# The tail of a two-layer image kernel: group-mean operations two strips later, the first turn one strip later, and loads of Fourier modes from the queues of ScalarE and SyncE

## The chip, the cores and the metric

The kernel runs on one core of one Trainium2 chip. The metric is the device time of one execution in microseconds (us); lower is better. The comparison is by the median of several executions.

## The reference

The input x is 4 images of 64 channels of 96 x 96 pixels, float32. Two layers are added to it, each on a group-normalized copy (32 groups, so two channels to a group):

```python
# layer 0: attention with a sigmoid over all 9216 pixels of an image, then a gate for each channel
out = einsum('bcm,bnm->bcn', V, sigmoid(Q^T K)) + v
x = x + out * sigmoid(mlp(mean(out)) + mlp(max(out)))[:, :, None, None]

# layer 1: a layer in Fourier space with 32 x 16 modes
u_hat = rfft2(gn(x))                           # two-dimensional transform of each channel
top = einsum('bchw,cohw->bohw', u_hat[:, :, :16, :16], W_pos)    # complex 64 x 64 mix per mode
bot = einsum('bchw,cohw->bohw', u_hat[:, :, -16:, :16], W_neg)
x = x + irfft2(modes of top and bot, all others zero)
```

## The kernel before, in words

The four images are worked on in two pairs. A pair has 2 x 64 channels, which fill the 128 partitions, and lies in SBUF as one tile of 128 x 9216. Attention over both pairs takes most of the execution: TensorE makes energies (line L572), ScalarE their sigmoids (L593), TensorE the products with the values (L610). The Fourier layer of pair 0 is hidden beside the attention of pair 1 (class `Hidden`). The Fourier layer of pair 1 has nothing to hide beside: it is the **tail**, the code from the pool "tail" on, and takes the last 86 us. The change lies there.

The tail has these stages, in order.

1. **Gate** (L641 to L656), a few small operations, and eight matmul instructions that only keep TensorE busy (`occupy`, L956; there are more such calls later).
2. **Strips.** The pair is cut into 12 strips of 8 image rows (128 x 768). For each strip, VectorE adds layer 0's result to the original x (`combine`, L178), except for the five strips in `ADDED` (4, 5, 6, 8, 10), where ScalarE scales (L975) and a GpSimd DMA accumulates (L976). VectorE then turns the strip (L983, into `xt`, one of four buffers), ScalarE sums its squares (L988), and TensorE makes the transform along the width with six instructions (L995). Strips 0 to 3 share the PSUM tile `pa_0`, 4 to 7 `pa_1`, 8 to 11 `pa_2`; when four are done, `rows_turned(n)` turns the tile on VectorE (L1001, into `a0`, `a1`, `a2`), and `rows(n)` makes the transform along the height (L1007).
3. **Group statistics** (`group_stats`). Means over two channels are made by a matmul with the matrix `pav`. For pair 1, `offset` is that matmul (L146, into the bank `pm`), a copy of its result (L147, into `mr`) and a difference (L148, `d`); `spread_out` (L151) and `third` (L155 to L158, with a power on GpSimd) follow when the variance is there. `spread` (L189 to L203) hands the result to the rows in the order of the modes.
4. **Modes.** VectorE and ScalarE write the modes to the tile `u` (L1042 to L1055). `mix(q, half)`, q from 0 to 7, multiplies four rows of modes by their weights (L225); `evacuate` copies the result from PSUM, in turn by VectorE (L125, half 0) and by ScalarE (L127, half 1). `moved` holds the last copy. For q below 6 the result goes to DRAM by a DMA of SyncE (L243, tensor `vd`) and returns in another layout into the tile `vt` (`back`, L278). The last two q (`NPICK`) never go to DRAM: `pick` moves them by matmuls (L261), and VectorE adds them to `vt` (L266), which needs every load of `vt`.
5. **Inverse transform**: along the height (L1097, `pz`), a turn by VectorE (L1104), along the width (L1114, `py`), the sum with x (L1122) and the stores, in turn from SyncE and ScalarE (L1123).

`back` issues four DMAs for each call, two images by two slots; slot 0 and slot 1 take the queues that it is given in turn. With `queues = (nc.sync, nc.gpsimd)`, the first call (16 rows, 64 KB each) puts all four on GpSimd and the second (8 rows, 32 KB each) two on SyncE and two on GpSimd.

Weights still missing when the tail begins are loaded during the strips: nine of 512 KB by GpSimd into the space of the squares (L1064, each behind the squares of the strips that it overwrites), and eight of 512 KB by SyncE into `a0`, `t0` to `t3`, `a1`, `a2` and `s` (L933, each behind the last matmul that reads its buffer).

The strips, the statistics and the modes stand in `tc.manual_schedule`: each engine takes its instructions in the order written. The mixing loop stands outside of it. `with tc.issue_after(ins)` keeps what is issued inside it on the engine of `ins` behind `ins`; it orders nothing on other engines.

Of the kernel before, what the change touches and what calls it, by code (L numbers as in the profile page):

```python
# [47 lines left out]
KH = 32  # L48
# [35 lines left out]
NPICK = 2  # L84
# [4 lines left out]
def tile_kernel(ctx: ExitStack, tc: tile.TileContext, x, cst, late, spec, out):  # L89
    nc = tc.nc  # L90
# [24 lines left out]
    def named(name, rows=P):  # L115
        return cs[:rows, PLACE[name]]

    pav, nhalf, low_sb, ident = named("pav"), named("nhalf"), named("low"), named("ident")
    turn, moved = [0], [None]

    def evacuate(dst, src):

        turn[0] ^= 1
        if turn[0]:
            moved[0] = nc.vector.tensor_copy(dst, src)  # L125
        else:
            nc.scalar.copy(dst, src)  # L127

    def group_stats(stats, bank, name):


        mv = small.tile([P, 2], F32, tag=f"mv_{name}", name=f"mv_{name}", bufs=1)
        mr = small.tile([P, 2], F32, tag=f"mr_{name}", name=f"mr_{name}")
        t = small.tile([P, 1], F32, tag="t", name=f"t_{name}")
        d = small.tile([P, 1], F32, tag="d", name=f"d_{name}")

        def first():
            nc.vector.bn_aggr(mv, stats.rearrange("p s k -> p (s k)"))

        def second():  # L140
            offset()
            spread_out()

        def offset():
            pm = bank(f"pm_{name}")
            nc.tensor.matmul(pm[:, 0:1], pav, mv[:, 0:1], start=True, stop=True)  # L146
            nc.vector.tensor_copy(mr[:, 0:1], pm[:, 0:1])  # L147
            nc.vector.tensor_tensor(d, mv[:, 0:1], mr[:, 0:1], ALU.subtract)  # L148

        def spread_out():  # L150
            nc.vector.scalar_tensor_tensor(t, d, d, mv[:, 1:2], ALU.mult, ALU.add)  # L151

        def third():
            pv = bank(f"pv_{name}")
            nc.tensor.matmul(pv[:, 0:1], pav, t, start=True, stop=True)  # L155
            ve = small.tile([P, 1], F32, tag="ve", name=f"ve_{name}")
            nc.vector.tensor_scalar(ve, pv[:, 0:1], GN_EPS, None, ALU.add)  # L157
            nc.gpsimd.tensor_tensor(mr[:, 1:2], ve, nhalf, ALU.pow)  # L158

        if stats is None:  # L160
            return mr, [offset, spread_out, third], mv
        return mr, [first, second, third], mv

    def normalize(dst, src, mr):
        nc.vector.tensor_scalar(dst, src, mr[:, 0:1], mr[:, 1:2], ALU.subtract, ALU.mult)

    class Layer1:
# [44 lines left out]
        def mix(self, q, half):  # L212

            pv = self.bank(f"pv_{self.p}_{q}_{half}")  # L220
            for k in range(2):
                kw = half * 2 + k
                for g in range(4):
                    at = ((4 * q + g) * KW + SIDE * kw) * 4
                    self.last = nc.tensor.matmul(  # L225
                        pv[bass.ts(g, 32), :].rearrange("q (n k o) -> q n k o", n=SIDE, o=C)[
                            :, :, k, :],
                        self.ut[:, at:at + 32],
                        self.wts[4 * q + g].rearrange("q (n k o) -> q n k o", n=SIDE, o=C)[
                            :, :, kw, :], start=True, stop=True)  # L230
            vm = self.vms[q].rearrange("q (n m) -> q n m", n=SIDE)
            self.move(vm[:, :, bass.ts(half, 2 * C)], pv.rearrange("q (n m) -> q n m", n=SIDE))
            if half == 0:
                return

            if self.p == 0:
                for g in range(4):
                    self.queues[0].dma_start(
                        self.vd[4 * q + g, :4 * SIDE], self.vms[q][32 * g:32 * g + 4 * SIDE, :])
                if q in (5, 7):  # L240
                    self.back(KH // 2 * (q == 7), KH // 2, self.queues[:1])
            elif q < KH // 4 - NPICK:
                self.queues[0].dma_start(  # L243
                    self.vd[4 * q:4 * q + 4].rearrange("h s m -> (h s) m")[:P - 4 * SIDE],
                    self.vms[q][:P - 4 * SIDE])
                if q == 3:
                    self.vt = self.place_of_vt()
                    nc.gpsimd.memset(self.vt, 0.0)
                    self.back(0, KH // 2, self.queues[1:])
                if q == KH // 4 - NPICK - 1:  # L250
                    self.back(KH // 2, KH // 2 - 4 * NPICK, self.queues)

        def pick(self, picks):

# [167 lines left out]
    with tc.tile_pool(name="work", bufs=1) as work, \  # L422
# [132 lines left out]
        def first_queries():  # L555


            pq = bank_a("pq_first")
            projected[0] = nc.tensor.matmul(pq, named("wq"), xs[0][:, :NB], start=True, stop=True)
            q = qp.tile([P, NB], F32R, tag="q", name="q_first")  # L560

            def splits():
                qu, qh = at[:, 12, :], at[:, 13, :].bitcast(F32R)
                both(qu, qh, pq, named("bq"))
                low_or_high(q, qu, qh, low_sb[:, 0:1])
            return q, splits
# [103 lines left out]
        with tc.manual_schedule(engines=ENGINES):  # L670
# [17 lines left out]
            q, split_queries = first_queries()  # L688
# [108 lines left out]
        while len(done) < len(sizes):  # L797
# [18 lines left out]
            elif total[t] < ALL:  # L816
                steps = together.setdefault(t, [])
# [94 lines left out]
        gate, steps, f = after(1)  # L912
# [7 lines left out]
    with tc.tile_pool(name="tail", bufs=1, reuse_waits="tile") as tail, \  # L920
# [6 lines left out]
        def place_of(tag, name):  # L927

            return tail.tile([P, KW * C], F32, tag=tag, name=name)
# [20 lines left out]
        def occupy(n, behind, pool):  # L950
# [3 lines left out]
            with tc.issue_after(behind.ins):  # L954
                for _ in range(n):
                    nc.tensor.matmul(pd, cs[:, :P], cs[:, :NB], start=True, stop=True)  # L956

        small_bank = psum("ps_m")
        l1 = Layer1(1, gate, lambda name: small_bank.tile([P, NB], F32, tag="m", name=name),
                    evacuate, (nc.sync, nc.gpsimd))  # L960
        l1.wts = wts
        occupy(4, projected[0], small_bank)
        x1 = xs[1]

        mr, steps, mv = group_stats(None, l1.bank, "l1_1")
# [32 lines left out]
        def rows_turned(n):  # L998

            a = place_of(f"a{n}", f"a_{n}")  # L1000
            nc.vector.transpose(a, along_w[n].rearrange("q (h c) -> q c h", c=SQ))  # L1001
            along_h[n] = a.rearrange("q (c s k) -> q s c k", s=2, k=KW)

        def rows(n):
            for part in range(2):
                for b in range(2):
                    nc.tensor.matmul(pu[b], fh[bass.ts(b, C), part, bass.ts(n, P)],  # L1007
                                     along_h[n][bass.ts(b, C), part],
                                     start=(n == 0 and part == 0),
                                     stop=(n == NSQ - 1 and part == 1))  # L1010
# [9 lines left out]
        with tc.manual_schedule(engines=ENGINES):  # L1020
            for s in range(NSTRIP):
                if s not in ADDED:
                    l1.combine(s, again[:, bass.ts(s, STRIP)])
                strip(s)
                if s == 1:
                    steps[0]()
                if s == 4:
                    rows_turned(0)
                    rows(0)
                if s == 9:  # L1030
                    rows_turned(1)
            var = small.tile([P, 1], F32, tag="var", name="var")
            nc.vector.tensor_reduce(var, squares, AX.X, ALU.add)
            nc.vector.tensor_scalar(mv[:, 1:2], var, 1.0 / N, None, ALU.mult)
            steps[1]()
            steps[2]()
            rows_turned(2)
            rows(1)
            rows(2)
            l1.spread(mr)  # L1040
            for b in range(2):
                nc.vector.transpose(t[:, bass.ts(b, NB)],  # L1042
                                    pu[b].rearrange("q (c k) -> q k c", k=KW))
            for half in range(2):
                h = bass.ts(half, KH // 2)
                for b in range(2):
                    nc.scalar.activation(u[:, :, :, h, 0, b], tb[b][:, :, :, h], AF.Copy,
                                         scale=l1.rs[:, 0, b:b + 1])
                    nc.vector.tensor_scalar(u[lo, :, :, h, 1, b], tb[b][hi, :, :, h],
                                            l1.rs[hi, 1, b:b + 1], None, ALU.mult)  # L1050
                    if b == 0:
                        nc.vector.tensor_scalar(u[hi, :, :, h, 1, b], tb[b][lo, :, :, h],
                                                l1.rs[lo, 0, b:b + 1], None, ALU.mult)
                    else:
                        nc.scalar.activation(u[hi, :, :, h, 1, b], tb[b][lo, :, :, h], AF.Copy,  # L1055
                                             scale=l1.rs[lo, 0, b:b + 1])
                if half == 0:
                    l1.constant_mode()
# [164 lines left out]
```

## Time and profile before

| what | us |
|---|---|
| median of 3 runs (lowest, highest) | 3034.89 (3033.67, 3035.25) |
| the profiled execution's own time | 3035.74 |
| its span in the profile | 3033.9 |
| start of the tail: attention's last matmul ends | 2948.19 |
| first combine, strip 0 (L178) | 2951.38 |
| last matmul of strip 11 ends (L995) | 2978.08 |
| mixing, first to last matmul of L225 | 2985.06 to 2999.08 |
| addition into `vt` starts (L266) | 3006.25 |
| inverse transform along the height starts (L1097) | 3007.77 |
| inverse transform along the width starts (L1114) | 3016.67 |

Times are microseconds from the start of the span. The profiled execution took 1.84 us more than its span, and 0.85 us more than the median. In a line of the trace's timeline the columns are the start, the duration, the engine, the line, the operation, output and input with their shapes, and how often; in brackets stands how long the engine was idle before, and what released it. POOL is GpSimd, DVE is VectorE, ACT is ScalarE, SP is SyncE, PE is TensorE and PEld its weight load. "SPq" or "POOL" with DMA_DIRECT2D is the issue of a DMA, not its transfer. PEclk is the TensorE clock that was granted, as a share of full speed.

### The profile page before, as it was taken

Reading aid. Unit: us, or ns where it says so; the run is one execution under the profiler, and the core shown is the slowest. Engines: PE = TensorE matmul, PEld = TensorE weight load, DVE = VectorE, ACT = ScalarE, POOL = GpSimd, SP = SyncE. Lnnn points to the kernel's source line nnn. Section 1 sums busy time; section 2 is a strip of 40 time slices with the busy share of each in tenths; the row PEclk is TensorE's granted clock in tenths of the full one; section 3 lists DMA queues with packets and bytes.
Section 4 is the critical chain, followed back from the end, with each engine's and each line's share of the span. In section 5 each row is a group of like instructions: output and inputs, shape, how many; then the busy total and the mean of one; then the engine's idle time right before and its main releaser. Section 6 shows DMA issues by size and latency. Waiting matters only on the chain.

```text
span 3033.9 us, 44107 instructions
## 1 busy us (share of the span) xinstructions
PE 3011.3 (99%) x19364; PEld 1114.1 (37%) x19364; DVE 308.4 (10%) x706; ACT 2416.9 (80%) x1555; POOL 73.1 (2%) x144
## 2 busy tenths in 40 slices
PE   9999999999999999999999999999999999999998
PEld 4333333333333333333433333333333333333336
DVE  6300000000000000002411101000000000000006
ACT  4788888888888888887788887778778888888872
POOL 0100000000000000001200000000001000000001
PEclk9999999999999999999999999999999999999999
DMA  4100000000000000001423222421113000000027
GB/s 160 31 4 4 4 4 4 4 4 4 4 1 4 4 4 4 4 4 37 108 53 78 76 79 88 132 39 39 56 41 125 4 4 4 4 4 4 6 68 238
DMA packets 114401, 117.09 MB, mean 39 GB/s; under 512 B 77520, under 2 KB 84496, under 8 KB 114112
## 3 DMA queue, kind: packets, MB, share of 16 engines
q1 hardware_dynamic: 105536, 92.82, 11.1%
q0 software_dynamic: 7664, 18.89, 2.0%
q8 instruction: 152, 2.49, 0.3%
q10 hardware_dynamic: 1008, 2.56, 0.2%
q14 instruction: 41, 0.34, 0.0%
HBM read 79.94 MB, written 32.31 MB: 37 GB/s over the span
## 4 chain that ended last, share of the span: by engine, by line
PE 97%; DVE 1%; DMA 1%; issue 0%; ACT 0%; SPq 0%; POOL 0%; DVEq 0%; POOLq 0%; ACTq 0%
PE banks L610 77%; PE banks L572 17%; PE banks L491 1%; PE banks L225 1%; DVE x L1122 0%; PE banks L413 0%; PE pa L995 0%; DMA x<-in_x_dram 0%; ACT at L593 0%; PE pv L225 0%; PE pz L1097 0%; PE banks L336 0%; PE pu L1007 0%; PE banks L456 0%; DVE xt L983 0%
## 5 line engine op out<-in xcount | busy, mean ns | idle before, releaser
L593 ACT ACTIVATE at<-banks 128x2048 f32<-128x2048 f32 (+1 forms) x1501 | 2388.3, 1642 | 532.0 <-PE banks L572 520.3
L610 PE MATMUL banks<-at,vT 128*64 128x512 f32 (+1 forms) x11824 | 2400.6, 546 | 0.0
L610 PEld LDWEIGHTS banks<-at,vT 128*64 128x64 f32 x11824 | 777.8, 136 | 1361.8 <-issue 1306.8
L572 PE MATMUL banks<-q,kT 32*128 32x512 f32 x5040 | 542.6, 452 | 0.8 <-ACT at L593 0.7
L572 PEld LDWEIGHTS banks<-q,kT 32*128 32x128 f32 x5040 | 223.7, 182 | 447.5 <-issue 337.4
L616 DVE SCALAR_TENSOR_TENSOR x<-banks,x 128x512 f32<-128x512 f32 x36 | 24.9, 691 | 2023.3 <-PE banks L610 1945.4
L542 POOL DMA_DIRECT2D stage<-qk x96 | 47.7, 504 | 930.6 <-DMA qk<-turned 928.8
L417 DVE TENSOR_TENSOR x<-banks,x 128x768 f32<-128x768 f32 x12 | 11.5, 958 | 168.5 <-PE banks L413 168.5
L491 PEld LDWEIGHTS banks<-cs,x 64*64 64x64 f32 x1152 | 21.8, 135 | 16.6 <-ACT at L593 11.5
L498 DVE TENSOR_TENSOR vT<-banks,cs 128x256 f32<-128x256 f32 x72 | 26.8, 413 | 0.0
L491 PE MATMUL banks<-cs,x 64*64 64x80 f32 (+1 forms) x1152 | 25.9, 234 | 0.0
L618 DVE TENSOR_REDUCE maxs<-x 128x1 f32<-128x512 f32 x36 | 24.7, 686 | 1.3
L624 DVE BATCH_NORM_STATS2 stats<-x 128x6 f32<-128x512 f32 x36 | 22.6, 681 | 3.7 <-DMA x<-in_x_dram 3.7
L728 DVE COPY ws<-banks 128x512 f32<-128x512 f32 x16 | 11.1, 692 | 115.3 <-PE banks L225 115.3
L158 POOL TENSOR_TENSOR mr_l<-ve_l,cs 128x1 f32<-128x1 f32 x4 | 2.2, 562 | 840.2 <-DVE ve_l L157 840.2
L995 PE MATMUL pa<-xt,lc 128*128 128x256 f32 x72 | 18.3, 410 | 3.0 <-DVE xt L983 3.0
L976 POOL DMA_DIRECT2D x<-vT x5 | 4.4, 1001 | 659.3 <-ACT x L975 659.3
L728 DVE COPY ae<-banks 128x512 f32<-128x512 f32 x6 | 4.2, 692 | 157.3 <-issue 114.9
L663 PE MATMUL banks<-x 128*128 128x256 f32 (+1 forms) x48 | 14.2, 451 | 4.9 <-DMA x<-in_x_dram 4.7
L572 PE MATMUL banks<-q_first,kT 32*128 32x512 f32 x144 | 17.1, 459 | 1.7 <-ACT at L593 1.1
L988 ACT ACTIVATE vT<-x,less 128x768 f32<-128x768 f32 x12 | 11.1, 926 | 9.4 <-DVE x L178 7.3
L529 DVE STREAM_TRANSPOSE turned<-t 128x384 f32<-128x384 f32 (+1 forms) x35 | 17.8, 510 | 1.2
(146 smaller groups left out, 440.7 us busy)
## 6 DMA issues: line engine op xcount, KB each, us to landing
ws<-in_spec_dram SPq DMA_DIRECT2D x20, 512.0 KB
q<-qk SPq DMA_DIRECT2D x280, 32.0 KB
x<-in_x_dram SPq DMA_DIRECT2D x17, 512.0 KB
out_dram<-x SPq DMA_DIRECT2D x17, 384.0 KB
room<-in_spec_dram SPq DMA_DIRECT2D x12, 512.0 KB
old<-in_x_dram SPq DMA_DIRECT2D x12, 384.0 KB
qk<-turned SPq DMA_DIRECT2D x96, 48.0 KB
x1d<-x SPq DMA_DIRECT2D x12, 384.0 KB
```

Of the source, the lines that this page charges most:

```text
L225: self.last = nc.tensor.matmul(pv[bass.ts(g, 32), :].rearrange("q (n k o) -> q n k o", n=SIDE, o=C)[:, :, k, :], self.ut[:, at:at + 32], s ...
L491: projected[0] = nc.tensor.matmul(pp[bass.ts(e, P // 2), b, 2 * a + h, :width], src[rows, a, h, bass.ts(e, P // 2)], named("wv")[rows, :wi ...
L498: nc.vector.tensor_tensor(vT[:, 4 * s:4 * s + 4, bass.ts(b, C)].rearrange("p (h a) m -> p a h m", h=2), pp[:, b, :, :C].rearrange("p (a h) ...
L529: nc.vector.transpose(turned[:, k:].rearrange("p k a (m h) -> p (k a) h m", h=2), t[:, k:].rearrange("p k a h m -> p (k a) h m").bitcast(F32))
L542: nc.gpsimd.dma_start(come[bass.ts(r, QK), :], split[p][s][:, r % 2, bass.ts(r // 2, NB // 2)])
L572: nc.tensor.matmul(banks[:, bank_of(i), :], kT[r:r + 32, i % TILES // 8, i // 4 % 2, :], ask[i // TILES][r:r + 32, :], start=True, stop=True)
L593: nc.scalar.activation(at[:, of:of + n, :], banks[:, bank:bank + n, :], AF.Sigmoid)
L610: attended[0] = nc.tensor.matmul(acc[half, cols], vT[:, j, half], at[:, place(2 * pair + b), cols], start=(j == 0), stop=(j == NCH - 1 and ...
L616: nc.vector.scalar_tensor_tensor(blk, acc, 1.0, blk, ALU.mult, ALU.add, accum_out=sums[p][:, m:m + 1])
L618: mark[0] = nc.vector.tensor_reduce(maxs[p][:, m:m + 1], blk, AX.X, ALU.max)
L624: each = [lambda s=s: nc.vector.bn_stats(stats[:, s, :], xs[p][:, bass.ts(s, NB)]) for s in range(NBLK)]
L995: nc.tensor.matmul(along_w[n][:, bass.ts(i, STRIP // NSQ)], fw[:, bass.ts(k, P)], v[:, k], start=(k == 0), stop=(k == NSQ - 1))
```

## The change

The matmul of `offset` becomes a step of its own, `shared`, which stays behind strip 1; the copy and the difference that remain in `offset` move behind strip 3. `rows_turned(0)` and `rows(0)` move from behind strip 4 to behind strip 5. In pair 1, the first call of `back` moves from behind `mix(3, 1)` to behind `mix(6, 1)` and the second from behind `mix(5, 1)` to behind `mix(7, 1)`; the queues become SyncE and ScalarE. So the first call's four DMAs are ScalarE's, behind ScalarE's copy for q = 6, and the second's are two of SyncE and two of ScalarE, the latter behind ScalarE's copy for q = 7. The clearing of `vt` (L248) stays where it is. The diff:

```diff
-    turn, moved = [0], [None]
+    turn, moved = [0], [None, None]
...
         if turn[0]:
             moved[0] = nc.vector.tensor_copy(dst, src)
         else:
-            nc.scalar.copy(dst, src)
+            moved[1] = nc.scalar.copy(dst, src)
...
         def second():
+            shared()
             offset()
             spread_out()
 
+        pm = []
+
+        def shared():
+            pm.append(bank(f"pm_{name}"))
+            nc.tensor.matmul(pm[0][:, 0:1], pav, mv[:, 0:1], start=True, stop=True)
+
         def offset():
-            pm = bank(f"pm_{name}")
-            nc.tensor.matmul(pm[:, 0:1], pav, mv[:, 0:1], start=True, stop=True)
-            nc.vector.tensor_copy(mr[:, 0:1], pm[:, 0:1])
+            nc.vector.tensor_copy(mr[:, 0:1], pm[0][:, 0:1])
             nc.vector.tensor_tensor(d, mv[:, 0:1], mr[:, 0:1], ALU.subtract)
...
         if stats is None:
-            return mr, [offset, spread_out, third], mv
+            return mr, [shared, offset, spread_out, third], mv
...
                 if q == 3:
                     self.vt = self.place_of_vt()
                     nc.gpsimd.memset(self.vt, 0.0)
-                    self.back(0, KH // 2, self.queues[1:])
-                if q == KH // 4 - NPICK - 1:
-                    self.back(KH // 2, KH // 2 - 4 * NPICK, self.queues)
+            if self.p == 1 and q >= KH // 4 - NPICK:
+                with tc.issue_after(moved[1].ins):
+                    if q == KH // 4 - NPICK:
+                        self.back(0, KH // 2, self.queues[1:])
+                    else:
+                        self.back(KH // 2, KH // 2 - 4 * NPICK, self.queues)
...
-                    evacuate, (nc.sync, nc.gpsimd))
+                    evacuate, (nc.sync, nc.scalar))
...
                 strip(s)
-                if s == 1:
-                    steps[0]()
-                if s == 4:
+                if s in (1, 3):
+                    steps[s // 2]()
+                if s == 5:
                     rows_turned(0)
                     rows(0)
...
-            steps[1]()
             steps[2]()
+            steps[3]()
             rows_turned(2)
```

## The prediction

> **What bounds the kernel now.** I began with the page's busy shares: TensorE has 99% of the span, but nearly all of that is attention, which the diff leaves alone. So I went to the chain that ended last, from 2948 us on, to see what carries the tail:
>
> ```profile
> 2954.86 2.59 PE pa L995 x12
> 2957.45 0.13 PE pm_l L146 x2
> ...
> 2957.61 0.17 DVE mr_l L147
> ...
> 2961.87 4.23 PE pa L995 x12
> 2966.10 0.04 issue
> 2966.14 1.99 PE pu L1007 x8
> ...
> 2981.83 0.33 PE pr L189 x8
> ```
>
> The columns are start, duration and what. The chain goes back and forth between TensorE and VectorE: neither is the bound of the strips, each waits for the other. The timeline names the waits:
>
> ```profile
> 2957.61 0.16 DVE L147 COPY mr_l<-pm_l 128x1 f32<-128x1 f32 x1 [1.97 <-PE pm_l L146]
> 2959.95 1.67 PE L995 MATMUL pa<-xt,lc 128*128 128x256 f32 x6 [2.38 <-DVE xt L983]
> 2961.87 4.23 PE L995 MATMUL pa<-xt,lc 128*128 128x256 f32 x12 [0.24 <-DVE xt L983]
> 2964.83 1.25 DVE L1001 STREAM_TRANSPOSE a<-pa 128x1024 f32<-128x1024 f32 x1 [2.16 <-PE pa L995]
> ```
>
> VectorE idles 1.97 us at the copy of `pm`, whose matmul stands behind the twelve of strips 0 and 1; TensorE then has no strip for 2.38 us; and VectorE idles 2.16 us for `pa_0`. The third line shows a cost that no wait shows: twelve instructions take 4.23 us here, against 2.59 above. The windows of 1 us (length; busy time of PE, PEld, DVE, ACT, POOL; then PEclk, DMA share, GB/s) say why:
>
> ```profile
> 2958.00:2959.00 1.00, 0.00 (x0) 0.00 (x0) 0.96 (x2) 0.08 (x1) 0.32 (x1) 1.00 1.10 194
> 2963.00:2964.00 1.00, 1.00 (x4) 0.82 (x3) 0.00 (x0) 1.00 (x3) 0.01 (x1) 0.50 1.16 151
> 2965.00:2966.00 1.00, 1.00 (x6) 0.62 (x4) 1.00 (x1) 0.00 (x0) 0.45 (x1) 1.00 0.91 314
> 3005.00:3006.00 1.00, 0.00 (x0) 0.00 (x0) 0.00 (x0) 0.00 (x0) 0.00 (x0) 0.83 0.03 8
> 3008.00:3009.00 1.00, 1.00 (x6) 1.00 (x8) 0.00 (x0) 0.00 (x0) 0.00 (x0) 0.50 0.00 0
> ```
>
> The idle TensorE lost half its clock from 2961.3 to 2964.7, and again from 3005.7 to 3012.4. The second loss follows the loads of `vt`:
>
> ```profile
> 2998.00 0.56 POOL L278 DMA_DIRECT2D vt<-vd  x1 [10.04 <-DMA vd<-vm]
> 3000.33 1.30 SPq L278 DMA_DIRECT2D vt<-vd  x2
> 3001.42 2.65 POOL L278 DMA_DIRECT2D vt<-vd  x5 [2.86 <-issue]
> 3006.25 1.42 DVE L266 TENSOR_TENSOR vt<-picked,vt 128x256 f32<-128x256 f32 x4 [7.28 <-DMA vt<-vd]
> ```
>
> GpSimd issues one load at 2998.00, stands 2.86 us with nothing shown as the cause, and issues the other five until 3004.07. The last, issued at 3003.51, lands 2.33 us later; only then does VectorE add. The picks were done at 3002.7, so this stage waits for GpSimd's queue alone.
>
> [...] the four switches (2961.34, 2964.69, 3005.67, 3012.45) lie 3.35, 40.98 and 6.78 us apart, multiples of 3.4. In both windows ahead of a drop TensorE was idle some 2.05 us. [...] the trace's SyncE loads moved their bytes by 3002.9, though no landing is shown for them. [...]
>
> **Part 1: `offset` behind strip 3, the first turn behind strip 5.** No operation is added or removed. I ran both queues forward with steps from this trace: combine to turn 1.01 us, turn to next 0.90, `rows_turned` 1.18, copy and difference 0.27 together; on TensorE 1.37 per strip at full clock (the first twelve instructions took 2.75 in the timeline) and 1.83 for `rows(0)` (half of the 3.63 to 3.70 of sixteen).
> VectorE: turn of strip 1 at 2954.66, combine 2 at 2955.56, turns of 2 and 3 at 2956.57 and 2958.48, copy at 2959.36 (its matmul was done at 2957.57: no wait), turns of 4 and 5 at 2959.63 and 2960.50, `rows_turned(0)` at 2961.37.
> TensorE: strip 2 from 2957.60, strip 3 from 2959.46 to 2960.83, which is before VectorE wants `pa_0`. TensorE's gap is 0.49 us in place of 2.38, so I expect no loss of clock. From there it is the bound: 9 strips at 1.37 and `rows(0)`, 14.16 us, from 2959.46 to 2973.62, against 2977.9 before. The matmul of the variance (L155) follows at once: **4.28 us earlier**. The accumulated strips don't stop this: issued from 2952.61 on, they land after 4.0 to 10.2 us, strip 4 by 2956.6, strip 6 by 2961.1, strip 10 by 2966.1, each ahead of its turn (2959.63, 2962.6, 2969.3). Moved past: ScalarE's squares and GpSimd's loads follow the strips and come earlier too. If that cover failed (an accumulation later), the cost would be its lateness, at most the 4.28.
>
> The loads of weights cannot come earlier in bulk: the DMA share is about 1 from 2965 to 2986. The only slack is 2973 to 2976, some 1.1 us at 410 GB/s. So they drain near 2985.4 (2986.5 less 1.1) and the last one, for `s`, near 2986.7. `mix` would then start at 2980.8 and want its last rows at 2992.8: covered by 6 us. But the writes to `vd`, 6 x 459 KB, would begin behind the drain and move some 0.32 MB per us (windows 2990 to 2993): 8.6 us, to 2995.3, and 0.9 to land. Unhindered, the last would land at 3000.30 - 4.28 = 2996.0. I take 0.5 us for this crowding, 0 to 2 as its bounds.
>
> **Part 2: the loads of `vt`.** Times here are before the shift of 4.28. ScalarE's copy for q = 6 ends at 2997.99, and the first four rows of `vd` landed at 2997.36, so its four issues start at once. No row shows ScalarE issuing small loads of 1 KB runs. Its stores (L1123) take 0.34 us each, SyncE's two loads of this kind 0.28 and 0.97, SyncE's 280 loads L550 0.30 to 2.00 with a median of 0.42. I take the median: 4 x 0.42 = 1.7 us, bounds 1.2 and 8.0. Queued behind them is ScalarE's copy for q = 7, for which `pick` waits: it moves from 2999.14 to 2999.7 and ends at 3000.3. TensorE is with the picks of q = 6 until 3000.87, so nobody waits. The second call's loads may go when the last `vd` row has landed (3000.30): SyncE's as before, ScalarE's at 3000.4 and 3000.8. SyncE's later one, issued at 3000.66, moved its bytes by 3002.9; with four at once I put the last landing at 3003.4. So L266 starts at 3003.45 instead of 3006.25: **2.8 us earlier**, 2.3 after the crowding. GpSimd loses six DMAs and nothing waits for it any more; late next is a tie of the loads and of the picks (3002.7).
>
> **Part 3: the clock.** TensorE would be idle from 3003.6 to 3004.9, 1.3 us and not 4.2, less than the 2.05 us that cost the clock. At full speed `pz` takes half its 6.13 us. VectorE's first turn then starts 1.05 us after TensorE instead of 2.07, and its eight turns run without their 0.39 us gap. Before `py` stand six busy-keeping instructions of 2.84 us that wait for about the fifth turn: 1.05 + 5 x 0.67 + 0.1 + 2.84 = 7.35 against 8.90 before. **1.5 us**, from 0 (clock lost again) to 2.5 (that wait is not binding). The last stage is VectorE's 13 sums and is unchanged.
>
> **Sum.** 4.28 + 2.3 + 1.5 = 8.1 us off the profiled execution: span 3025.8, time 3035.74 - 8.1 = 3027.6. That execution stood 0.85 above the median, so from 3034.89 I get 3026.8.
>
> **Rivals.**
> - *Part 1 alone holds.* ScalarE's issues take 0.97 each: its copy ends at 3002.5, the picks at 3004.4, the second call's loads land near 3005.2; 0.9 us minus crowding is gained and the clock falls again. 3034.89 - 4.3 - 0.4 = 3030.2. For it: SyncE's 0.97 on this very kind of load. Against it: stores at 0.34. Likewise 3030.6 if nothing but the strips moves.
> - *The transfers give the 4.28 back.* If the drain of weights, not TensorE, sets when `vd` lands, 3000.30 stays and only parts 2 and 3 count: 3034.89 - 2.8 - 1.5 = 3030.6. For it: the share of 1 to 2986. Against it: `mix` never waits for a weight, and the last write is bound by its own issue.
> - *Slower: ScalarE's queue becomes the bound.* With d for an issue, L266 starts at 2997.99 + 6d + 0.58 (the copy) + 1.7 (landing). It breaks even with 3006.25 at d = 1.0, and with the strips' 4.28 at d = 1.71. At the longest SyncE issue seen, 2.00, it starts at 3012.3, 6.0 later than before: 3034.89 - 4.28 + 6.0 = 3036.6. For it: nothing shows this queue in such use. Against it: a mean at the worst of 280.
> - *It doesn't do what it says:* the mixing loop is outside the written order, so the planner may put ScalarE's copy for q = 7 ahead of the first loads. Then all six follow 2999.72, the last landing is near 3004.3 and 1 us of the gain is lost: 3027.8.
>
> **How the numbers follow.** The full case with the planner's variant 0.61 (3024.8 to 3028.8), the two rivals near 3030.5 together 0.30, one in six of that at 3028.8 or less when a part of the clock is kept, ScalarE's queue 0.09. About 0.2%, 6.07 us, is what a measurement can tell from no change; the border is 3028.8. Faster: 0.61 + 0.05 = 0.66. Slower by over 0.2% (3041.0) needs d above 2.7: 0.04 of the 0.09. Within: 0.30. The range reaches from the full case's low end (strips 4.4, loads 3.3, clock 2.4) to 3031.2, beyond the rivals near 3030.5.
>
> **What would show it.** Right: no idle of VectorE at L147 and L1001, PEclk 1.00 from 2957 to 2966; L155 near 2973.6; L225 starting near 2980.8; eight `vt` issues on ACTq and SPq, four behind the copy for q = 6; L266 near 2999.7, L1097 near 3001.1 with PEclk 1.00, L1114 near 3008.5. Wrong: ACT copies of L127 late by over 1.2 us with the picks waiting for them, weights awaited by L225, or `vd` landing as late as 3000.

## The result, and the profile after

The median of 18 runs fell from 3035.06 to 3028.64 us; the ratio is 0.998, with a 95% interval from 0.9973 to 0.9988. That is 6.4 us or 0.21%, inside the range that was forecast and 1.8 us slower than the forecast number. By the interval the gain is 3.6 to 8.2 us: that the kernel became faster is clear of noise, that it did so by more than 0.2% is not. The profiled execution has a span of 3027.4 us and took 3029.19, so it stands 0.55 above the median. The changed kernel's runs lie from 3027.40 to 3031.39 in two groups, nine up to 3028.09 and nine from 3029.19 on. The median falls into the gap between them, where no run stands; one run more in either group would move it by 0.55 us.

The same chain of waits as before, from the strips on (start, duration, what; line numbers are those of the changed kernel, up to eight higher):

```profile
2961.12 0.05 DVE mr_l L152
2961.17 0.00 issue
2961.17 4.15 PE pa L1003 x18
2965.32 1.92 PE pu L1015 x8
2967.24 2.80 PE pa L1003 x12
...
2982.69 14.02 PE pv L230 x256
2996.71 3.65 PE picked L269 x16
3000.36 0.87 PE idle_I-15684_15689 L964 x2
```

Where 12 instructions of L1003's counterpart took 4.23 us, 18 now take 4.15. The timeline shows the two waits gone and the loads on their new queues:

```profile
2961.04 0.12 DVE L152 COPY mr_l<-pm_l 128x1 f32<-128x1 f32 x1
2963.03 1.21 DVE L1009 STREAM_TRANSPOSE a<-pa 128x1024 f32<-128x1024 f32 x1
2975.55 0.28 PE L160 MATMUL pv_l<-t_l,cs 128*128 128x1 f32 x2
2995.33 1.99 ACTq L286 DMA_DIRECT2D vt<-vd  x4
2997.36 0.58 ACT L127 COPY w_early<-pv 128x512 f32<-128x512 f32 x1 [1.74 <-PE picked L269]
2997.67 0.81 ACTq L286 DMA_DIRECT2D vt<-vd  x2
2997.77 0.63 SPq L286 DMA_DIRECT2D vt<-vd  x2
3001.34 1.42 DVE L274 TENSOR_TENSOR vt<-picked,vt 128x256 f32<-128x256 f32 x4 [4.75 <-PE idle_I-15684_15689 L964]
3002.86 3.92 PE L1105 MATMUL pz<-vt,gh_in_fours 64*128 64x256 f32 x32 [1.64 <-DVE vt L274]
3003.99 4.90 DVE L1112 STREAM_TRANSPOSE z<-pz 128x512 f32<-128x512 f32 x8 [1.24 <-PE pz L1105]
3006.71 2.84 PE L964 MATMUL idle_I-15718_15732<-cs 128*128 128x512 f32 x6
```

No bracket stands behind the copy and the turn: VectorE no longer waits there. ScalarE's four issues take 1.99 us and end at 2997.32; its copy for q = 7 follows at 2997.36 (its bracket names the picks, but it stands behind these issues in ScalarE's queue), and the two SyncE issues go when the last row of `vd` has landed. The windows (the third column from the right is the granted clock) hold the surprise:

```profile
28.00:29.00 1.00, 1.00 (x6) 0.27 (x4) 0.00 (x0) 1.00 (x1) 0.00 (x0) 0.50 0.24 59
2963.00:2964.00 1.00, 1.00 (x6) 0.89 (x5) 1.00 (x2) 0.92 (x3) 0.54 (x1) 1.00 1.05 187
3004.00:3005.00 1.00, 1.00 (x12) 0.94 (x11) 1.00 (x2) 0.00 (x0) 0.00 (x0) 1.00 0.00 0
```

In the tail the clock is full as long as TensorE works, as forecast (1.00 in every window of 1 us from 2950 to 3020). But it was halved at 28 us, where the first profile of before had 1.00, and all that follows came late: attention's last matmul ended at 2949.81 instead of 2948.16. From there to the end of the span the tail took 85.74 us before and 77.59 after, 8.15 less, almost the 8.1 of the sum. The medians differ by 6.4. The experiments ask where the difference comes from.

### The profile page after: what moved, and what is told of

The parts are those of the page before. It is cut to its first block, busy times and chain, and to the rows that moved or that the text cites. A ratio compares the mean times of both kernels' runs of the same rounds, so it can differ in the third digit from the quotient of the medians.

```text
span 3027.4 us, 44108 instructions
## 1 busy us (share of the span) xinstructions
PE 3009.2 (99%) x19364; PEld 1111.5 (37%) x19364; DVE 308.1 (10%) x706; ACT 2416.8 (80%) x1555; POOL 69.8 (2%) x138
## 3 DMA queue, kind: packets, MB, share of 16 engines
q0 software_dynamic: 7472, 18.56, 2.0%
q10 hardware_dynamic: 1408, 2.88, 0.3%
## 4 chain that ended last, share of the span: by engine, by line
PE 98%; DVE 1%; DMA 0%; ACT 0%; issue 0%; SPq 0%; POOL 0%; DVEq 0%; ACTq 0%
PE banks L618 77%; PE banks L580 17%; PE banks L499 1%; PE banks L230 1%; PE pv L230 0%; DVE x L1130 0%; PE banks L421 0%; DMA x<-in_x_dram 0%; PE pa L1003 0%; ACT at L601 0%; PE banks L344 0%; PE pu L1015 0%; PE banks L464 0%; DVE xt L991 0%; DVE x L183 0%
## 5 line engine op out<-in xcount | busy, mean ns | idle before, releaser
L170 DVE TENSOR_SCALAR x<-x,mr_l 128x512 f32<-128x512 f32 x36 | 17.6, 530 | 0.7 <-POOL mr_l L163 0.7
L1003 PE MATMUL pa<-xt,lc 128*128 128x256 f32 x72 | 16.8, 385 | 0.6 <-DVE mr_l L152 0.4
```

## The experiments

Stages are measured in each profile: *strips* from the first combine to the variance's matmul, *loads* from the start of mixing to the addition into `vt`, *pz* from the first matmul of the transform along the height to that along the width, *stores* from the last sum to the end of the span. *Attention* is the end of its last matmul, and *tail* is the time from there to the end of the span. Every line is one execution. Each text set apart below is what was expected of an experiment: a theory, and its rivals.

| profile | attention | tail | strips | loads | pz | stores |
|---|---|---|---|---|---|---|
| before | 2948.16 | 85.74 | 26.53 | 21.19 | 8.83 | 5.44 |
| after | 2949.81 | 77.59 | 22.52 | 18.65 | 6.62 | 6.05 |
| before again | 2949.89 | 84.61 | 26.24 | 20.75 | 8.31 | 5.56 |
| after again | 2949.90 | 77.90 | 22.52 | 18.89 | 6.62 | 6.13 |
| strips' part alone | 2948.17 | 81.93 | 22.51 | 20.99 | 9.12 | 5.55 |
| loads' part alone | 2948.25 | 81.75 | 26.24 | 19.12 | 6.71 | 5.93 |
| before, busy behind the picks | 2948.17 | 84.23 | 26.07 | 20.77 | 6.43 | 5.88 |
| before, pair near 25 us | 2948.15 | 83.75 | 25.17 | 20.58 | 8.31 | 5.93 |
| after, pair near 25 us | 2948.47 | 77.63 | 22.51 | 18.70 | 6.62 | 6.04 |
| the same, trimmed | 2948.65 | 78.25 | 22.51 | 18.91 | 6.93 | 6.15 |
| after, early places | 2949.90 | 81.50 | 22.52 | 22.97 | 6.62 | 5.64 |
| after, SyncE alone | 2949.72 | 82.18 | 22.52 | 20.37 | 9.36 | 6.18 |
| after, first turn at strip 4 | 2948.52 | 78.08 | 22.83 | 18.61 | 6.62 | 6.27 |
| after, pair near 25, two behind the picks | 2948.36 | 77.64 | 22.52 | 19.07 | 6.62 | 5.68 |

**Both kernels once more**, unchanged.

> The kernel before, unchanged, for a second profile. In its first profile the tail took 85.7 us from the last attention matmul to the end; in the changed kernel's profile 77.6, so 8.2 us less, though the medians of all runs differ by 6.4. Theory A (chance of the clock): [...] the same kernel loses it in other places in another execution; this tail then differs from 85.7 by over 0.5 us, and a stage with a clock of 0.50 has moved, gone or been added. Theory B (fixed): the tail is again 85.7 within 0.3 us and the difference to the medians comes only from the 1.5 us lost near 27 us in the changed kernel's profile.

> The changed kernel, unchanged, for a second profile. In its first one TensorE ran at half clock from 26.8 to 31 us, which the kernel before did not in its own, and everything from there to the tail came 1.65 us later. Theory A: the loss at 27 us is chance, and this profile need not have it; the attention then ends near 2948.2 as before. Theory B: it belongs to the changed program, and attention ends again near 2949.8. Both expect a tail of 77.6 us within 0.5[...].

The kernel before again, windows:

```profile
28.00:29.00 1.00, 1.00 (x4) 0.24 (x2) 0.00 (x0) 1.00 (x1) 0.00 (x0) 0.50 0.24 59
2963.00:2964.00 1.00, 1.00 (x4) 0.81 (x3) 1.00 (x2) 1.00 (x3) 0.12 (x1) 0.50 1.07 200
3008.00:3009.00 1.00, 0.24 (x2) 0.27 (x3) 0.66 (x2) 0.00 (x0) 0.00 (x0) 1.00 0.02 8
3010.00:3011.00 1.00, 1.00 (x6) 0.84 (x6) 1.00 (x2) 0.00 (x0) 0.00 (x0) 0.50 0.00 0
```

Now the kernel before has the early half clock too, ends attention at 2949.89, and has a tail 1.1 us shorter than in its first profile. Its second loss begins between 3009 and 3010, behind the start of the transform along the height at 3008.76 and not 2.1 us ahead of it. Theory A holds for the tail of before. What repeats is the length of the losses: 3.35 and 6.78 us in the first profile of before, 3.42 near 28 us in that of the changed kernel (worked out from the clock of its windows at 26 and 30 us, 0.84 and 0.95), and, worked out in the same way, 3.40 to 3.42 or 6.82 in the five experiments below whose windows show both ends. So each loss is as long as one or two steps of about 3.4 us, while its place in the work differs between the executions. The changed kernel's second profile has the early loss again (attention ends at 2949.90, which is what its Theory B said); since the kernel before now has it too, it does not belong to the changed program alone. Its tail, 77.90, is what both theories expected.

**Each part alone.** The strips' part alone keeps the old loads; the loads' part alone keeps the old strips:

```diff
 # strips' part alone, against the changed kernel: the two calls of back as in the kernel before, and
-                    evacuate, (nc.sync, nc.scalar))
+                    evacuate, (nc.sync, nc.gpsimd))
 # loads' part alone, against the kernel before: back behind mix(6, 1) and mix(7, 1), and
-                    evacuate, (nc.sync, nc.gpsimd))
+                    evacuate, (nc.sync, nc.scalar))
```

> Only the part in the strips: offset behind strip 3, first turn behind strip 5; loads of vt as before, from GpSimd and SyncE. The prediction's sum gives it 4.3 us (4.0 in the changed kernel's profile, from first combine to the variance's matmul), so a ratio near 0.9986 and a median near 3030.8. Rival (clock is part of the price): of the 4.3 us some 1.5 is the half clock from 2961 to 2965 in the one profile of before, and executions without it gain only 2.5 to 3, a ratio near 0.9991.

> Only the part in the loads: back behind mix 6 and 7, from ScalarE and SyncE; strips as before. The prediction's sum gives it 2.3 us for the loads and 1.5 for the clock in the transform along the height, 3.8 in all, a ratio near 0.9987. Rival (clock by chance): executions of before that keep the clock there gain 2.5 only, a ratio near 0.9992. If the two parts are independent, the gains of this kernel and of the strips alone add up to that of both, about 6 to 6.4 us.

Medians of 13 runs: 3032.64 and 3033.09, against 3035.11; both ratios are 0.9993, with intervals from 0.9985 to 1.0001 and to 1.0002. So 2.5 and 2.0 us, near the rivals and below the sum's 4.3 and 3.8; but the intervals reach from no gain to one of 4.6 us, so they don't exclude the sum's values either. The two gains add up to 4.5 us, not to the 6 to 6.4 that were expected of independent parts; intervals this wide leave open whether the parts need each other. By stages they are independent: each brings its own stage about to the length that it has in the changed kernel (22.51, and 19.12 where the profiles with both parts have 18.6 to 19.1) and leaves the other as before. What they do not fix is the clock: the strips' part alone had its pz at 9.12, the longest but one, with a clock of 0.50 from 3003 to 3008, and the loads' part alone still lost the clock in the strips, where 13 instructions took 4.20 us (12 take 2.86 at full clock, as a profile below shows).

**The clock by itself**: the kernel before with TensorE kept busy behind the picks.

```diff
-        occupy(1, l1.last, mix_bank)
+        occupy(7, l1.last, mix_bank)
```

> The kernel before, with seven pairs of busy-keeping matmuls behind the picks instead of one, so that TensorE is not idle while VectorE waits for the loads; nothing else. Theory (the clock is a part of the gain by itself): PEclk stays 1.00 through the transform along the height, from its first matmul to that along the width 6.6 us instead of 8.3 to 9.1, the addition still starts with the loads, and the median falls by about 2 us, to 3033. Rival (the addition waits for the busy-keeping matmuls too, as the changed kernel's profile says of its one pair): it starts a little later than the loads, and the gain shrinks to 1.5 or less. Rival (the clock isn't the cause of the 2.2 us): the stage keeps its 8.3 to 9.1.

The median was 3035.46, ratio 0.9999 (0.9991 to 1.0008): no gain that can be told, where 2 us were expected. The timeline of this kernel says why:

```profile
3002.12 6.17 PE L956 MATMUL idle_I-15684_15689<-cs 128*128 128x512 f32 x14
3005.38 1.42 DVE L266 TENSOR_TENSOR vt<-picked,vt 128x256 f32<-128x256 f32 x4 [6.86 <-DMA vt<-vd]
3008.22 3.72 PE L1097 MATMUL pz<-vt,gh_in_fours 64*128 64x256 f32 x32
```

The theory's mechanism is there: at full clock (1.00 in every window from 3000 to 3020) the 32 instructions take 3.72 us instead of 6.13, and pz 6.43. But my fourteen instructions ran 6.17 us, beyond the addition, and the transform waited 1.3 us behind them. I had taken too many; so this run prices the clock at 1.9 to 2.4 us in pz, of which 0.6 to 1.1 would be left behind that wait, too little for the medians to show. The addition starts while they run: it doesn't wait for them.

**The early loss.** One pair of matmuls into a bank that the next energies overwrite, at a time when TensorE waits for the first sigmoids (1.06 us in the first profile of before), in the kernel before and in the changed one:

```diff
             values_of(0, 1)()
+            warm(0, NB)
```

> The kernel before, with one pair of busy-keeping matmuls near 25 us, where TensorE idles for the first sigmoids. Theory (the early half clock is chance, worth 1.65 us where it strikes): PEclk is 1.00 from 22 to 40 us, attention ends at 2948.2, and the runs lie closer together than the 3032.5 to 3037.6 of before; the median falls by 0.3 to 1 us. Rival: the spread has another cause and stays.

> The changed kernel with the same pair near 25 us. Theory: attention ends at 2948.2, the two groups of run times (3027.4 to 3028.1, and 3029.2 to 3031.4) become one near 3027.5, and against the kernel before with the same pair it is faster by the 7.4 us that four profiles give for the tail (85.7 and 84.6 before, 77.6 and 77.9 after). Rival (the tail's gain is really about 6): the difference of the two is 6 us or less.

The clock is 1.00 at 28 us in both, and attention ends at 2948.15 and 2948.47. All four profiles with the pair end it by 2948.65; of the ten without it five end it at 2949.72 or later. Medians: 3034.49 and 3028.11, so 6.4 us between the two, and the tails of 83.75 and 77.63 differ by 6.1: nearer to the rival's 6 than to the theory's 7.4. The changed kernel's 9 runs lie from 3027.71 to 3029.99, not in one group yet: two stand near 3029.9. The kernel before went from 3035.22 to 3034.49, not clear of noise (ratio 0.9997, 0.9989 to 1.0005), and its 13 runs still spread over 4.1 us against 5.2 of 33 runs without the pair, so most of its spread has another cause, as the rival said. Here the tail of the kernel before was the shortest of the three seen, and this is what it looks like:

```profile
2957.60 0.16 DVE L147 COPY mr_l<-pm_l 128x1 f32<-128x1 f32 x1 [1.97 <-PE pm_l L146]
2959.94 1.56 PE L996 MATMUL pa<-xt,lc 128*128 128x256 f32 x6 [2.38 <-DVE xt L984]
2961.86 2.86 PE L996 MATMUL pa<-xt,lc 128*128 128x256 f32 x12 [0.35 <-DVE xt L984]
2963.45 1.25 DVE L1002 STREAM_TRANSPOSE a<-pa 128x1024 f32<-128x1024 f32 x1 [0.79 <-PE pa L996]
```

TensorE was idle for the same 2.38 us as in the kernel before, yet the clock stayed full (1.00 at 2961 and at 2963), and the twelve instructions took 2.86 us, not 4.23. VectorE's second wait shrank from 2.16 to 0.79. So of the 4.0 us that the strips' part takes from the first profile, 1.36 go with the clock and 2.66 (25.17 less 22.51) are there without it.

**Fewer busy-keeping matmuls ahead of the last transform**, on top of the pair near 25 us:

```diff
-        occupy(3, last, py_bank)
+        occupy(1, last, py_bank)
```

> The same as the changed kernel with the pair near 25 us, and one pair of busy-keeping matmuls instead of three ahead of the transform along the width. In the changed kernel's profile these six instructions end at 3009.5, 0.6 us after VectorE's last turn at 3008.9. Theory: that transform starts right behind the last turn, 0.5 us sooner, and the median is 0.5 us under that of the kernel with three. Rival: TensorE's idle time there costs the clock, the sums of the last stage come later, and it is slower by 1 us or more.

The median was 3028.02, ratio to the kernel before 0.9974 (0.9965 to 0.9984), against 3028.11 and 0.9977: no difference that can be told. The profile can't be compared by its length, since this execution lost the clock at about 3003.1, ahead of the edit, early in a transform along the height before which TensorE had been idle for 1.9 us:

```profile
3004.00:3005.00 1.00, 1.00 (x8) 1.00 (x7) 0.80 (x2) 0.00 (x0) 0.00 (x0) 0.50 0.00 0
```

The theory's first half is there: the transform along the width starts at 3008.88, 0.06 us behind VectorE's last turn, and so pz is 6.93 in spite of the lost clock.

**The old places with the new queue**: in the changed kernel, `back` again behind `mix(3, 1)` and `mix(5, 1)`, without `issue_after`.

```diff
-            if self.p == 1 and q >= KH // 4 - NPICK:
-                with tc.issue_after(moved[1].ins):
...
+                    self.back(0, KH // 2, self.queues[1:])
+                if q == KH // 4 - NPICK - 1:
+                    self.back(KH // 2, KH // 2 - 4 * NPICK, self.queues)
```

> The changed kernel with ScalarE and SyncE as queues, but back at its old places (behind mix 3 and mix 5) and without the order behind ScalarE's copies. The planner then puts the first call's four loads behind ScalarE's copy for q = 4, ahead of that for q = 5. Theory (the places matter because ScalarE's waiting issue holds its copies): the loads wait for the fourth row of vd, which lands 12.3 us after mixing starts; four issues of 0.5 follow; the copies for q = 5, 6 and 7 come 3.5 us late, with them the last write to vd, and L274's counterpart starts 21 to 22 us after the start of mixing, not 18.7 to 18.9. Rival (the queue alone makes the gain): 18.7 to 19.2 here too.

ScalarE's rows:

```profile
2991.67 0.58 ACT L127 COPY w_early<-pv 128x512 f32<-128x512 f32 x1 [1.12 <-PE pv L230]
2995.76 2.67 ACTq L283 DMA_DIRECT2D vt<-vd  x4
2998.47 1.56 ACT L127 COPY w_early<-pv 128x512 f32<-128x512 f32 x3 [6.21 <-DMA vt<-vd]
3002.16 0.81 ACTq L283 DMA_DIRECT2D vt<-vd  x2
```

ScalarE stands 6.2 us between its copies, three of them come at once, the last write to `vd` goes 16.31 us after the start of mixing instead of 11.23, and the addition starts 22.97 us after it. The theory's direction and its mechanism hold; its 21 to 22 was too low, because the wait ended at 13.0, not 12.3, and an issue took 0.67. TensorE waited 2.80 us for those copies, and its clock was halved during the picks (0.50 from 3001 to 3003), which took 5.41 us instead of 3.72; but the addition starts 3.6 us after the second call's first issue, as in the changed kernel (3.7), so it is the loads that set it. In this stage the queue alone costs 2 us against before (22.97 against 21.19); with the new places it gains 2 (18.65 to 18.89).

**The new places with SyncE alone**:

```diff
-                    evacuate, (nc.sync, nc.scalar))
+                    evacuate, (nc.sync, nc.sync))
```

> The changed kernel with all eight loads of vt on SyncE. The planner puts one load of the first call between the writes to vd for q = 4 and q = 5. Theory (it waits for the fourth row's landing, 12.3 us after mixing starts, and holds the last write by 1.2 us): that lands near 16.4, four more issues of 0.4 to 0.6 follow, and the addition starts 20 to 21 us after the start of mixing. Rival (any hardware queue does it): 18.7 to 19.2, as with ScalarE.

SyncE's rows:

```profile
2992.11 0.30 SPq L248 DMA_DIRECT2D vd<-w_early  x1
2995.67 0.32 SPq L286 DMA_DIRECT2D vt<-vd  x1
2996.10 0.36 SPq L248 DMA_DIRECT2D vd<-w_early  x1
2996.51 4.16 SPq L286 DMA_DIRECT2D vt<-vd  x7
```

The first load sits waiting between the two last writes, holds the second until 13.51 us after the start of mixing (11.23 in the changed kernel), and the addition starts at 20.37, inside the theory's 20 to 21. What the rival calls a hardware queue stands in the list of queues of the two first profiles: from before to after, q0, named software_dynamic, falls from 18.89 to 18.56 MB and q10, named hardware_dynamic, rises from 2.56 to 2.88 MB, by about the 0.33 MB of the six loads that went from GpSimd to ScalarE; SyncE's transfers are in q1, hardware_dynamic too. So it is not enough to take any hardware queue. `issue_after` orders nothing on SyncE, since it names ScalarE's copy; whether SyncE would do with its loads kept behind the last write was not tried.

**The first turn back behind strip 4**, the rest as changed:

```diff
-                if s == 5:
+                if s == 4:
```

> The changed kernel with the first turn back behind strip 4: of the strips' part only the offset moves. From the first combine to the variance's matmul the kernel before took 26.2 to 26.5 us with half clock near 2961 and 25.2 without it, the changed one 22.5. Theory (the two edits take away one wait each): the offset gives back its 2.0 us wait and the clock, the turn still waits for TensorE, and the stage takes 22.9 to 23.5. Rival (the turn's wait came from the late strips 2 and 3, so it is gone with the offset's): 22.5 to 22.7, the second edit is worth nothing.

```profile
2961.49 1.25 DVE L1009 STREAM_TRANSPOSE a<-pa 128x1024 f32<-128x1024 f32 x1 [0.53 <-PE pa L1003]
```

The strips took 22.83 us, 0.31 more than with the turn behind strip 5, between the rival's 22.5 to 22.7 and the theory's 22.9 to 23.5. VectorE's wait for `pa_0` is still there, 0.53 us of the 2.16. So in this one profile the offset's move does nearly all of it, and most of the turn's wait came from the late strips 2 and 3, as the rival said, but not the whole.

**A version that keeps the clock**: the pair near 25 us and one more pair behind the picks.

```diff
-        occupy(1, l1.last, mix_bank)
+        occupy(2, l1.last, mix_bank)
```

> The changed kernel with the pair of busy-keeping matmuls near 25 us and a second pair behind the picks, so that TensorE's idle time ahead of the transform along the height is 0.7 us instead of 1.6. Theory (an idle time of 1.6 us loses the clock in some executions, as the trimmed kernel's profile shows, and the addition doesn't wait for these matmuls): the runs near 3030 are gone, the median is 3027.5 to 3028, and the stage from that transform to the next is 6.6. Rival (the addition waits for them): it starts 0.9 us later, and the median is 3028.5 or more.

```profile
2998.74 1.88 PE L965 MATMUL idle_I-15685_15690<-cs 128*128 128x512 f32 x4
3000.30 1.42 DVE L274 TENSOR_TENSOR vt<-picked,vt 128x256 f32<-128x256 f32 x4 [5.17 <-DMA vt<-vd]
```

The median of 9 runs was 3027.77, ratio 0.9974 (0.9964 to 0.9984), and they lie from 3027.40 to 3028.27, as the theory said. The addition began at 3000.30 while the second pair ran until 3000.62, so it doesn't wait for it. TensorE was idle for 1.21 us ahead of the transform, not 0.7, and pz is 6.62. The idle time that lost the clock in the trimmed kernel's profile was 1.90 us; that 1.6 does it too was my estimate and is not shown. The median is 0.9 below that of the changed kernel, and its slowest run is faster than half of the changed kernel's; but the two were measured at different times, and the intervals of their ratios overlap. That it is the second pair that takes the runs near 3030 away is not shown: without it, with the pair near 25 us, they were two of nine, and in the trimmed kernel, also without it, none of nine.

## Why the prediction was right, and where its size was off

- **The strips.** Right in every step: the turn of strip 3 was forecast at 2958.48, 7.10 us after the start of the first combine (2951.38), and measured at 2960.14, 7.11 after 2953.03; TensorE back to back from there; no wait at the copy. Measured 4.01 and 3.72 us in the first two pairs of profiles, against 4.28; the forecast counted the clock lost there as a part of the gain, and against the profile that kept it the part is worth 2.66. The missing 0.3 of the first pair is for the most part the last strip, for which TensorE waits after all (0.23 us): VectorE and TensorE end nearly together.
- **Crowding of the DMA engines.** The first pair shows none: SyncE's wait for the last row of `vd` ends 15.08 us after the start of mixing, against 15.27 before. But over all profiles with the copies on time it ends after 14.6 to 15.3 with the loads at their old places (five profiles, mean 14.89) and after 15.1 to 15.6 with them at the new ones (seven, mean 15.35). So some 0.5 us is lost after all, and not for the reason given: the strips' part alone has 14.70, the loads' part alone 15.63. It goes with the loads' new places, not with the weights that were moved; how is not shown.
- **The loads.** 2.8 forecast ahead of that crowding and 2.3 with it, 2.54 measured in the first pair and 2.1 as a mean of three profiles of each kernel, with and without the pair near 25 us (20.8 before, 18.7 after). ScalarE's issue, the unknown, was 0.50 us against the 0.42 chosen from SyncE's loads, far below the 1.71 at which the slower rival would have broken even; its copy for q = 7 started 14.67 us after mixing, forecast 14.64. The planner kept the order.
- **The clock.** 1.5 forecast; 2.21 and 1.69 measured. The sum let the six busy-keeping instructions ahead of `py` wait for about the fifth turn, 4.50 us after the start of `pz`. They do not wait for it: they start at 3006.71, 3.85 us after that start and right behind the last `pz` matmul (3006.78), and pz is 6.62 and not 7.35. Nor do the 32 `pz` instructions take half of 6.13 us: 3.72 to 4.01 in the profiles with full clock there. The other step, that idle time below 2.05 us (TensorE's in the 3.4 us ahead of each of the first profile's two drops) keeps the clock, is refuted as a bound. It held in the changed kernel's own tails (1.64 and 1.88 us idle; forecast 1.3), but 1.90 us lost the clock in the trimmed kernel and 2.10 kept it with the loads' part alone, and near 25 us an idle time of 1.07 us was followed by half clock. So what kept the clock in these tails is not shown.
- **The stores** were put down as unchanged, with VectorE's 13 sums as the last stage. The sums are unchanged (10.62 and 10.63 us); the time behind the last one is 5.4 to 6.3 us in the profiles, 6.1 in the mean of the changed kernel's first two against 5.5. What decides that is open.
- **What was off is the sum's base.** It took one profile's losses of the clock for a fixed price, and took 8.1 us from the median as if every execution paid it. The tail of before was 85.74, then 84.61, then 83.75 in the version with the pair near 25 us, and the forecast was made from the dearest of the three. The changed kernel's three are 77.59, 77.90 and 77.63. So the three pairs differ by 8.15, 6.71 and 6.12 us, 7.0 in the mean. That the first came so near to 8.1 is in part luck: 4.01, 2.54 and 2.21, less 0.61 for the stores, stand where the sum had 4.28, 2.3, 1.5 and nothing. Whether the early loss of 1.65 us makes up the rest of the distance to 6.4 is not shown. It struck one of four profiles made from the kernel before without the pair and four of six made from the changed kernel, too few to tell; and with the pair in both kernels the medians still lie 6.4 us apart. The interval of the ratio, 4.5 us wide, holds 7.0 as well as 6.4.
- **The rivals.** That the transfers give the gain back, and that ScalarE's queue becomes the bound, are refuted by the profile after: mixing starts 29.7 us after the first combine and not 33.7, and the wait for the last row of `vd` ends 44.7 us after it and not 49.0. That only the strips' part holds is refuted by the stage of the loads (18.65 against 21.19), not by the median, whose interval of 3.6 to 8.2 us holds a gain of 4.3. The bound by ScalarE's queue comes true when the order behind the copies is taken away: 22.97 us for the loads, 1.8 more than before.

## What to carry to other kernels

Where a wait of one engine makes the next one wait, look for the small operation at its head: moving a copy of 0.16 us two strips later took away 1.97 us of VectorE's waiting and 2.0 of TensorE's (2.38 to 0.35), and in all nine profiles with it the strips' matmuls keep the pace that they have at full clock (18 in 4.15 us or 12 in 2.86). Put loads that wait for a late write on the queue of an engine that has nothing left to hold, behind its last urgent instruction: on ScalarE's the addition then started 18.65 us after mixing instead of 21.19, and with the same queue at the wrong place 22.97, 4 us later. And before a profile's half clock goes into a sum, take a second profile of the same kernel. In the four profiles with a pair of busy-keeping matmuls in the idle time near 25 us the clock was 1.00 at 28 us, in five of the ten without it 0.50; fourteen matmuls that overran their idle time made the next stage wait 1.3 us.

## What the runs showed of the hardware that was not expected

- The length of TensorE's idle time alone did not decide whether its clock fell: near 2960 an idle time of 2.38 or 2.39 us was followed by half clock in four profiles with the strips of the kernel before (0.50 at 2963 in the two of the kernel before; 13 instructions in 4.20 us and 14 in 4.80 in the other two) and left it at 1.00 in the fifth; ahead of the transform along the height 1.90 us halved it once while 1.88 and 2.10 did not; near 25 us, where TensorE was idle for 1.06 us in one piece in the first profile of before and for 1.07 in that of the changed kernel, it stayed at 1.00 in the former and fell to 0.50 in the latter, as in five of the ten profiles without the pair. One and the same stage, the strips of the kernel before, varied by 1.4 us with it (25.17 to 26.53).
- GpSimd stands 2.86 us between its first and second load of `vt` in every profile that has them: 2.85 or 2.86 in five of five. No run shows what this time is.
- The trace after named the busy-keeping matmuls as the releaser of the addition (4.75 us), as did two more profiles (4.79 and 4.70). The version with two pairs, where it started ahead of their end, shows that the name was an inference: it doesn't wait for them. That it waits for the loads instead fits the other eleven profiles, which name `vt<-vd`; the trace of the changed kernel gives no landing for the loads on the queues of ScalarE and SyncE.
